# A graph-attention kernel: stores of the transformed keys by halves of the partitions, and the first loads in another order

## The chip, the cores and the metric

The kernel runs on one core of one Trainium2 chip. The metric is the time of one execution on the device in microseconds (us); shorter is better. Three executions of the kernel before were timed, with a median of 545.88 us, and one more was recorded by the hardware profiler. Every view of the trace below is of that recorded execution.

A core has TensorE (PE, matrix products; its weight loads are listed apart as PEld), VectorE (DVE), ScalarE (ACT), GpSimd (POOL) and SyncE (SP). Sixteen transfer engines move data between DRAM and SBUF, the on-chip memory, which has 128 partitions. PSUM is the memory that TensorE writes its products to. A transfer is issued by an engine (nearly all of them by SP, a few by ACT) and goes into that engine's queue; SPq and ACTq in a row mean that the issuing is meant.

## The reference

The reference is one layer of graph attention in float32, with an integer adjacency. B = 16 graphs, N = 512 nodes of F = 512 features, L = 11 labels, 16 heads of 32 features, and the first 20 nodes as neighbours. Per graph it computes this:

```
self_feat = concat(v, q, but 0 for q where a row of v sums to 0) @ W_self.T + b_self
output    = self_feat
for d in 0, 1:                                   # the adjacency and its transpose
    cond, vb = sum of A over labels, A @ w_bias + b_bias
    qh  = self_feat @ Wq[d].T + bq[d]            # 512 queries
    kh  = self_feat[:20] @ Wk[d].T + bk[d]       # 20 keys
    aff = qh . kh / sqrt(32) by heads, -9e15 where cond <= 0, + vb
    w   = softmax(aff over the 20)
    output += (w @ self_feat[:20]) @ Wout[d] by heads + bout[d]
return v + relu(output)
```

## The kernel before, in words

The kernel has a setup for all graphs (the first 92 us or so), and then a loop of 16 passes, one for each graph, whose order of work is written out as a table of steps. The change touches the setup alone.

The setup turns everything that depends on the 20 neighbours into operands that the loop only has to load. It first warms TensorE with matrix products of ones (L581, result unused), while the first loads come in. The rows of the 20 x 16 neighbours (`xkv`) and the weights of the self features (`ws_v`) come in four pieces of 128 input features, k = 0 to 3; `kv_rows(k)` issues the piece of `xkv` on SP and that of `ws_v` on ACT. The products of piece k (`kv_terms`, L637) write four PSUM banks (ps_kv twice, ps_u, ps_v in the profile). The query's part follows (L656), then the keys' features (`key_rows`, L693), of which the differences to neighbour 0 are kept in `khD`.

Then come the **bursts**. `keys(runs)` multiplies the query weights into the keys (L790), so that the loop can multiply self features by the outcome without forming queries. The outcome has 16 stages, numbered `at_g`. A stage is collected in a tile `st` of 128 partitions x 2,128 float32 (14 graphs x 152); the first two graphs' part goes to another tile, `g01`, and stays on the chip. ACT (L811) and DVE (L813) evict the PSUM tiles of a burst into `st`. The pool has four `st` tiles, so the evictions of stage k use the tile of stage k - 4. When a stage is complete, SP stores it to DRAM with one transfer (`g_d`, L816). Each partition's 8,512 bytes are contiguous in DRAM. The loop loads its graph's part back from there (`load_keys`, L137).

Between the bursts, `plan` puts the values' products (`values`, L759, stored at L767 to `vw_d`), the masks of graph 0, the row sums, and the first feature products (L277). The engines get their instructions in the order of the program text, and each executes its own in that order, with semaphores between the engines. Transfers of one queue are also issued in order. The semaphores for transfers come in eight lanes that are used in turn, so a transfer that is issued waits for the landing of the one eight before it.

At the end of the setup its pools are given back, and the loop's tiles take over their memory: the sums of keys (L394, on POOL), for instance.

Of the kernel before, what the change touches and what calls it, by code (L numbers as in the profile page):

```python
# [14 lines left out]
P = 128  # L15
# [4 lines left out]
def gat_kernel(  # L20
# [20 lines left out]
    nc = tc.nc  # L41
# [13 lines left out]
    HA = 2  # L55
    RA = P // HA
# [6 lines left out]
    HF = F // 2  # L63
# [16 lines left out]
    def bank(name, at=0):  # L80
        if at % C > 1:
            return (ps_u, ps_v)[at % C - 2]
        return acc["pool"].tile([P, 512], F32, tag="acc", name=name)
# [3 lines left out]
    ws_v = const.tile([P, C, F], F32, name="ws_v")  # L87
# [13 lines left out]
    g_d = dram.tile([C * C, P, B - 2, WD // C], F32, name="g_d")  # L101
# [304 lines left out]
    def score_product(b, n):  # L406

        rows, keys, to = {
            1: (lambda: self_block(b, 0, 0), lambda: key_block(b, 0), ps_a),
            2: (lambda: self_block(b, 0, 1), lambda: key_block(b, 1), ps_w),  # L410
            3: (lambda: sums[b, "s", 4], lambda: key_block(b, 2), ps_e),
            4: (lambda: self_block(b, 1, 1), lambda: sums[b, "t", 4], ps_a),
            5: (lambda: sums[b, "s", 1], lambda: sums[b, "t", 1], ps_e),
            6: (lambda: sums[b, "s", 2], lambda: sums[b, "t", 2], ps_a),
            7: (lambda: sums[b, "s", 3], lambda: key_block(b, 3), ps_a),
        }[n]
        rows, keys, to = rows(), keys(), grid(to).rearrange("p j (x m) -> p j x m", m=NG)
        for k in range(2):
            for j in range(C):
                for a in range(HA):  # L420
                    nc.tensor.matmul(  # L421
                        to[bass.ts(a, RA), j, :, 1:], rows[:, k, bass.ts(j, RA)],
                        keys[:, k, a].rearrange("p (x m) -> p x m", m=ND),
                        start=False, stop=k == 1, skip_group_check=True,
                    )
# [118 lines left out]
    with tc.tile_pool(name="setup", bufs=1) as sp, tc.tile_pool(  # L544
# [6 lines left out]
        q_sb = sp.tile([P, C, B], F32, name="q_sb")  # L551
        bs_sb = sp.tile([P, C], F32, name="bs_sb")
# [11 lines left out]
        with tc.tile_pool(name="setup_k", bufs=1) as sk:  # L564
            xkv = sk.tile([P, C, BM], F32, name="xkv")
# [11 lines left out]
                nc.gpsimd.memset(mean[bass.ts(q, 32), q], 1.0 / 32)  # L577

            warm = bank("ps_warm")
            for _ in range(7):  # L580
                nc.tensor.matmul(warm[:, :P], ones, ones, start=True, stop=True)  # L581

            def rows(sb, src, queue=nc.sync):
                queue.dma_start(sb, src.rearrange("(c p) f -> p c f", p=P))

            def kv_rows(k, queue=nc.sync):
                rows(xkv[:, k : k + 1], xkvT[bass.ts(k, P)])
                rows(ws_v[:, k : k + 1], wsT[bass.ts(k, P)], queue)
# [9 lines left out]
                    wq[d].rearrange("(a l p) f -> p a l f", l=2, p=P)[:, :, l],  # L598
                )

            for k in range(3):
                kv_rows(k, nc.scalar)
                if k == 1:
                    nc.sync.dma_start(q_sb, qT)
            nc.scalar.dma_start(bs_sb, b_self)
            nc.scalar.dma_start(bk_sb, bk)
            nc.scalar.copy(nzk[:, :1], ones[:, :1])
            rows(xkv[:, 3:], xkvT[bass.ts(3, P)])
# [114 lines left out]
        with tc.tile_pool(name="setup_g", bufs=4) as sg:  # L723
# [55 lines left out]
            def keys(runs):  # L779


                pairs = [ps_s.tile([P, 2, 512], F32, tag="s", name=f"ps_g{runs[0]}{i}") for i in range(2)]
                at = 0
                for at_g, d, lo, hi in runs:
                    fc, hg = ORDERED[at_g]
                    n = (hi - lo) * ND
                    for hl in range(HL):
                        r = bass.ts(hl, DH)
                        for a in range(HA):
                            nc.tensor.matmul(  # L790
                                pairs[hl // 2][bass.ts(a, RA), hl % 2, at : at + n],
                                wq_sb[r, d, hg, bass.ds(fc * P + a * RA, RA)],
                                khD[r, d * C + hg, lo * ND : hi * ND], start=True, stop=True,
                            )
                    at += n
                at = 0
                for at_g, d, lo, hi in runs:
                    n = (hi - lo) * ND
                    if at_g not in stages:
                        stages[at_g] = sg.tile([P, B - 2, HL, 2, ND], F32, tag="st", name=f"st{at_g}")  # L800
                    st = stages[at_g]
                    for half in range(2):
                        of = pairs[half][:, :, at : at + n].rearrange("p h (b m) -> p h b m", m=ND)
                        to = st[:, max(lo - 2, 0) : hi - 2, bass.ts(half, 2), d].rearrange("p b h m -> p h b m")
                        evictions = [(to, of[:, :, max(2 - lo, 0) :])]
                        if lo == 0:
                            to = g01[:, :, at_g].rearrange("p b (h d m) -> p h b d m", d=2, m=ND)
                            evictions.append((to[:, bass.ts(half, 2), :, d], of[:, :, :2]))
                        for to, of in evictions:
                            if half == 0:  # L810
                                nc.scalar.activation(to, of, AF.Copy, scale=SCALE)  # L811
                            else:
                                nc.vector.tensor_scalar(to, of, SCALE, None, ALU.mult)  # L813
                    at += n
                    if d == 1 and hi == B:
                        nc.sync.dma_start(g_d[at_g], st)  # L816

            def features(n):
                if n == 1:
# [33 lines left out]
            for n, runs in enumerate(bursts):  # L853
                for i in range(len(rest)):
                    if i < (4 if n == 0 else 1) or any((d, ORDERED[at_g][1]) == rest[0] for at_g, d, _, _ in runs):
                        key_rows(*rest.pop(0))
                keys(runs)
                if 0 < n < 5:
                    for d in range(2):
# [422 lines left out]
```

## Time and profile before

| what | value |
|---|---|
| timed runs | 545.64, 545.88 and 546.28 us (median 545.88) |
| the recorded execution | 546.29 us, of which its span is 544.5 us |
| granted TensorE clock | 0.995 |
| busy in the span | PE 537.3 us, DVE 455.9, POOL 430.9, ACT 369.2 |
| stores of stages | 16 of 1,064 KB, issued from 29.4 to 86.5 us |

A row of the timeline reads: start in us, duration in us, engine, line, operation, output<-inputs, how many of them, and in brackets the idle time before it with what ended it. A row of the waits reads: engine, tile and line, what it waited for, us in total, how often, the longest. A row of the windows gives the stretch, its length, the busy time of PE, PEld, DVE, ACT and POOL (with the number of instructions), then the clock, the share of time for which the 16 transfer engines were busy on average, and GB/s. A row of a queue (q1 is SP's, q8 TensorE's instructions) has packets, MB and the share of the 16 engines' time.

### The profile page before, as it was taken

What the parts mean: (1) busy time and instruction counts of PE and PEld (TensorE: products, weight loads), DVE (VectorE), ACT (ScalarE), POOL (GpSimd) and SP (SyncE); (2) the same over time, 40 slices, a digit from 0 to 9 for tenths busy, and PEclk for the clock granted to TensorE, in tenths of its full rate; (3) what the DMA queues carried; (4) which work ended last, traced back from release to release, by engine and by line L of the source; (5) the groups of instructions that cost most, each with busy time, mean ns of one, the idle gap of its engine ahead of it and who ended that gap; (6) DMA issues with size and microseconds to landing.
All of it is one profiled execution on the core that took longest, in us unless ns stands there. A gap on an engine that the chain in (4) does not pass through costs nothing.

```text
span 544.5 us, 19552 instructions
## 1 busy us (share of the span) xinstructions
PE 537.3 (99%) x8136; PEld 415.4 (76%) x8136; DVE 455.9 (84%) x773; ACT 369.2 (68%) x804; POOL 430.9 (79%) x379
## 2 busy tenths in 40 slices
PE   9999999999999999999999999999999999999996
PEld 5444446988797979797978788887879797979794
DVE  0588674899989898989898988989898989898986
ACT  1145444767786869695968686968777786867554
POOL 3215906859797979797979798998979797979795
PEclk9999999999999999999999999999999999999998
DMA  8998989795575858585766656666657575745025
GB/s 296 396 413 332 362 330 330 230 304 171 184 234 185 260 171 266 169 245 194 221 222 187 235 179 216 213 196 213 195 200 234 195 248 182 224 128 172 23 79 194
DMA packets 87400, 122.90 MB, mean 226 GB/s; under 512 B 11656, under 2 KB 56208, under 8 KB 85264
## 3 DMA queue, kind: packets, MB, share of 16 engines
q1 hardware_dynamic: 86304, 120.47, 66.7%
q8 instruction: 64, 1.05, 0.8%
q10 hardware_dynamic: 1008, 1.19, 0.6%
q14 instruction: 24, 0.20, 0.1%
HBM read 84.99 MB, written 37.95 MB: 226 GB/s over the span
## 4 chain that ended last, share of the span: by engine, by line
PE 97%; DMA 0%; DVE 0%; POOL 0%; issue 0%; ACT 0%; DVEq 0%; POOLq 0%
PE ps_a L421 23%; PE ps_u L277 20%; PE ps_v L277 15%; PE ps_e L421 11%; PE ps_w L421 6%; PE ps_w L513 6%; PE ps_v L759 4%; PE ps_k L693 2%; PE ps_a L988 2%; PE ps_kv L637 1%; PE ps_e L513 1%; PE ps_v L693 1%; PE ps_u L693 1%; PE ps_warm L581 1%; DMA out_T<-o 0%; PE ps_u L637 0%
## 5 line engine op out<-in xcount | busy, mean ns | idle before, releaser
L485 POOL TENSOR_TENSOR s<-s,sm 128x640 f32<-128x640 f32 x60 | 76.3, 1274 | 40.4 <-DVE sm L481 40.3
L342 ACT ACTIVATE prod<-adj,wb_sb 128x160 f32<-128x160 int32 x165 | 80.5, 586 | 0.6 <-DMA adj<-in_adj 0.6
L538 POOL TENSOR_TENSOR o<-o,x 128x512 f32<-128x512 f32 x59 | 75.3, 1279 | 0.8 <-ACT o L1120 0.8
L476 ACT ACTIVATE s<-s 128x640 f32<-128x640 f32 x60 | 42.4, 730 | 25.4 <-DVE s L472 25.4
L277 PE MATMUL ps_u<-t,ws_s 128*64 128x246 f32 x480 | 55.0, 370 | 0.0
L449 DVE TENSOR_TENSOR u<-ps_a,both 128x640 f32<-128x640 f32 x30 | 24.7, 823 | 28.7 <-PE ps_a L421 28.7
L480 DVE TENSOR_REDUCE sm<-s 128x32 f32<-128x640 f32 x60 | 47.7, 796 | 0.0
L394 POOL TENSOR_TENSOR k<-g,k 128x608 f32<-128x608 f32 x30 | 44.0, 1488 | 1.1
L404 POOL TENSOR_TENSOR s<-sf 128x512 f32<-128x512 f32 x30 | 37.8, 1277 | 6.5 <-DVE sf L315 5.6
L277 PEld LDWEIGHTS ps_u<-t,ws_s 128*64 128x64 f32 x480 | 34.0, 137 | 11.7
L491 DVE STREAM_TRANSPOSE wt<-s 128x512 f32<-128x512 f32 x60 | 41.3, 689 | 0.1
L366 ACT COPY both<-add 64x160 f32<-64x160 f32 (+1 forms) x68 | 21.5, 316 | 24.1 <-DVE add L355 23.5
L243 POOL TENSOR_TENSOR t<-x 128x492 f32<-128x492 f32 x30 | 37.3, 1244 | 0.0
L394 POOL TENSOR_TENSOR k<-g 128x608 f32<-128x608 f32 x15 | 22.3, 1486 | 18.6 <-DMA g_d<-st 18.6
L513 PE MATMUL ps_e<-wt,vd 32*32 32x256 f32 (+1 forms) x600 | 36.6, 389 | 0.0
L513 PE MATMUL ps_w<-wt,vd 32*32 32x256 f32 (+1 forms) x600 | 36.6, 389 | 0.0
L315 DVE TENSOR_TENSOR sf<-ps_v,f 128x492 f32<-128x492 f32 x45 | 30.0, 667 | 6.7 <-PE ps_v L277 5.9
L347 DVE TENSOR_REDUCE cond<-adj 128x160 f32<-128x1760 int32 (+1 forms) x17 | 31.1, 1829 | 4.3 <-DMA adj<-in_adj 4.3
L243 POOL TENSOR_TENSOR t<-x,t 128x492 f32<-128x492 f32 x30 | 34.6, 1152 | 0.2
L421 PEld LDWEIGHTS ps_a<-g,sf 128*64 128x64 f32 x480 | 30.3, 137 | 5.6 <-issue 5.4
L175 ACT ACTIVATE xn<-xn 128x512 f32<-128x512 f32 x56 | 34.5, 618 | 0.0
L355 DVE TENSOR_REDUCE add<-prod 128x160 f32<-128x1920 f32 (+1 forms) x17 | 34.5, 2028 | 0.0
(366 smaller groups left out, 1516.8 us busy)
## 6 DMA issues: line engine op xcount, KB each, us to landing
g_d<-st SPq DMA_DIRECT2D x16, 1064.0 KB
g<-g_d SPq DMA_DIRECT2D x56, 304.0 KB
out_T<-o SPq DMA_DIRECT2D x60, 256.0 KB
xn<-in_xn SPq DMA_DIRECT2D x28, 512.0 KB
x<-in_xT SPq DMA_DIRECT2D x28, 512.0 KB
adj<-in_adj SPq DMA_DIRECT2D x32, 440.0 KB
nz<-nz_d SPq DMA_DIRECT2D x16, 256.0 KB
vd<-bd_d SPq DMA_DIRECT2D x64, 64.0 KB
```

Of the source, the lines that this page charges most:

```text
L243: nc.gpsimd.tensor_sub(t, one, two)
L277: nc.tensor.matmul(to[bass.ts(a, RA), bass.ts(i, HN)], lhs, x[:, k], start=n in starts and (i, k) == (0, 0), stop=k == 1, skip_group_check ...
L342: nc.scalar.activation(label_sums(b)[:, :, l], labels(b)[:, :, l], AF.Copy, scale=wb_sb[:, l : l + 1])
L394: op(t, one(), two())
L404: op(t, one(), two())
L421: nc.tensor.matmul(to[bass.ts(a, RA), j, :, 1:], rows[:, k, bass.ts(j, RA)], keys[:, k, a].rearrange("p (x m) -> p x m", m=ND), start=Fals ...
L476: nc.scalar.activation(t, t, AF.Exp)
L480: nc.vector.tensor_reduce(sm, rows_of(b, i, l), AX.X, ALU.add)
L485: nc.gpsimd.tensor_mul(t, t, us.pop((b, "sum", i, l)).unsqueeze(2).to_broadcast([P, 32, NG]))
L491: nc.vector.transpose(wts[b][:, i, l, : W * 4 // 5], t[:, :, :MW])
L513: nc.tensor.matmul((ps_w, ps_e)[a][to, g, bass.ts(c, NH)].rearrange("p (i j n) -> p i j n", i=2, n=32), lhs, rhs, start=False, stop=True, ...
L538: nc.gpsimd.tensor_add(t, t, xs[b][:, c])
```

## The change

There are three edits. One warming matrix product is dropped (7 become 6). The first loads are written out in another order: piece 0 of `xkv`, piece 0 of `ws_v` in two halves of its columns, the query `q_sb` and the bias `bs_sb`, and then pieces 1 and 2; before, `q_sb` came after piece 1 and `bs_sb` after piece 2. And each stage is stored by two transfers of 64 partitions each (HA is 2, RA is 64, HF is 256). Lines move by two or three: L637 becomes L639, L790 becomes L792, L816 becomes L819.

```diff
--- before.py
+++ after.py
@@ -577,7 +577,7 @@
                 nc.gpsimd.memset(mean[bass.ts(q, 32), q], 1.0 / 32)
 
             warm = bank("ps_warm")
-            for _ in range(7):
+            for _ in range(6):
                 nc.tensor.matmul(warm[:, :P], ones, ones, start=True, stop=True)
 
             def rows(sb, src, queue=nc.sync):
@@ -598,11 +598,13 @@
                     wq[d].rearrange("(a l p) f -> p a l f", l=2, p=P)[:, :, l],
                 )
 
-            for k in range(3):
+            rows(xkv[:, :1], xkvT[:P])
+            for h in range(2):
+                rows(ws_v[:, :1, bass.ts(h, HF)], wsT[:P, bass.ts(h, HF)], nc.scalar)
+            nc.sync.dma_start(q_sb, qT)
+            nc.scalar.dma_start(bs_sb, b_self)
+            for k in (1, 2):
                 kv_rows(k, nc.scalar)
-                if k == 1:
-                    nc.sync.dma_start(q_sb, qT)
-            nc.scalar.dma_start(bs_sb, b_self)
             nc.scalar.dma_start(bk_sb, bk)
             nc.scalar.copy(nzk[:, :1], ones[:, :1])
             rows(xkv[:, 3:], xkvT[bass.ts(3, P)])
@@ -813,7 +815,8 @@
                                 nc.vector.tensor_scalar(to, of, SCALE, None, ALU.mult)
                     at += n
                     if d == 1 and hi == B:
-                        nc.sync.dma_start(g_d[at_g], st)
+                        for a in range(HA):
+                            nc.sync.dma_start(g_d[at_g, bass.ts(a, RA)], st[bass.ts(a, RA)])
 
             def features(n):
                 if n == 1:
```

What moves at the start on ACT, which issues the loads of `ws_v`. Before:

```order
L584 DMA ws_v<-in_wsT 128x512 x3
L605 DMA bs_sb<-in_b_self 128x4
L606 DMA bk_sb<-in_bk 128x8
L607 ACT_TABLE_LOAD
L607 COPY nzk<-ones 128x1
```

With the change:

```order
L584 DMA ws_v<-in_wsT 128x256 x2
L605 DMA bs_sb<-in_b_self 128x4
L584 DMA ws_v<-in_wsT 128x512 x2
L608 DMA bk_sb<-in_bk 128x8
L609 ACT_TABLE_LOAD
L609 COPY nzk<-ones 128x1
```

The first load is now two of half the columns, and the small `bs_sb` stands ahead of pieces 1 and 2. On SP `q_sb` likewise moves from behind the second piece of `xkv` to behind the first.

The last stores on SP, ahead of the loads of graph 1's adjacency (`adj`), of its rows (`xn`) and of the label bias (`cq`). Before:

```order
L816 DMA g_d<-st_1133 128x2128
L767 DMA vw_d<-ws_q 128x4x128
L816 DMA g_d<-st_1183 128x2128
L816 DMA g_d<-st_1225 128x2128
L767 DMA vw_d<-ws_q 64x4x128 x2
L816 DMA g_d<-st_1271 128x2128
L125 DMA adj_1377<-in_adj 128x880 x2
L119 DMA xn_0_1380<-in_xn 128x1024
```

With the change:

```order
L819 DMA g_d<-st_1145 64x2128 x2
L769 DMA vw_d<-ws_q 128x4x128
L819 DMA g_d<-st_1196 64x2128 x2
L819 DMA g_d<-st_1239 64x2128 x2
L769 DMA vw_d<-ws_q 64x4x128 x2
L819 DMA g_d<-st_1286 64x2128 x2
L125 DMA adj_1393<-in_adj 128x880 x2
L119 DMA xn_0_1396<-in_xn 128x1024
```

Nothing changes places here; each store is issued twice, and what follows stands behind two transfers.

## The prediction

> **What bounds the kernel now.** I read the page first (shares of the engines, then the chain that ended last), then the waits of TensorE, then the stretches in which TensorE stands.
>
> ```profile
> span 544.5 us, 19552 instructions
> PE 537.3 (99%) x8136; PEld 415.4 (76%) x8136; DVE 455.9 (84%) x773; ACT 369.2 (68%) x804; POOL 430.9 (79%) x379
> PE 97%; DMA 0%; DVE 0%; POOL 0%; issue 0%; ACT 0%; DVEq 0%; POOLq 0%
> PE ps_a L1065 <- DVE wt L1029: 1.6, 1, 1.6
> PE ps_warm L581 <- DVE ones L569: 1.0, 1, 1.0
> PE ps_v L759 <- issue: 0.9, 1, 0.9
> ```
>
> TensorE is busy for 99% of the span and makes up 97% of the chain. Its three visible waits sum to 3.5 us. So a change that leaves TensorE's work alone can win very little, but it loses, one for one, every microsecond for which TensorE has to stand. All three edits lie in the setup, the first 92 us or so; nothing after it is touched.
>
> One of the three waits is of use here. It is put down to "issue", so no semaphore ended it:
>
> ```profile
> 62.15 1.91 PE L759 MATMUL ps_v<-wo_sb,kvT 128*32 128x512 f32 x12
> 64.95 1.05 PE L759 MATMUL ps_v<-wo_sb,kvT 128*32 128x512 f32 x4 [0.89 <-issue]
> 65.93 0.29 PE L790 MATMUL s_g(10, 0, 12, 16)0_1030<-khD,wq_sb 32*64 32x76 f32 x4
> 69.79 1.92 PE L759 MATMUL ps_v<-wo_sb,kvT 128*32 128x512 f32 x16
> 71.64 0.48 PE L790 MATMUL ps_g(12, 0, 0, 16)0_1115<-khD,wq_sb 32*64 32x304 f32 x4
> ```
>
> The same sixteen records take 1.85 us from 69.79 to 71.64, but 3.78 us from 62.15 to 65.93: 1.93 us are lost in the middle of a group. TensorE's own instructions come through a transfer queue too, and the records show one block of them arriving just then:
>
> ```profile
> q8 instruction: 64, 1.05, 0.8%
> 0.00:64.90 64.90, 63.02 (x1102) 30.93 (x1103) 39.31 (x107) 23.06 (x72) 28.89 (x36) 1.00 0.97 360
> 36.40:92.15 55.75, 54.86 (x979) 26.69 (x970) 39.38 (x104) 25.14 (x81) 26.73 (x23) 1.00 0.91 343
> ```
>
> These are 64 blocks of 16 KB (1.05 MB). The last two rows end in the share of time for which the 16 transfer engines worked, and in GB/s: 0.97 up to the stall, and 0.91 at 343 GB/s from the first key store's bytes (36.40) to the last one's landing (92.15), as the packets' records have them. I read the lost 1.93 us as TensorE running out of instructions because their block was held up by full transfer engines. The second row says what matters most below: **in the stretch of the key stores the transfer engines are nearly as full as TensorE.**
>
> **The stores in halves.** Sixteen stores of 1,064 KB become 32 stores of 64 partitions each. There are two costs. The issuing cost comes first:
>
> ```profile
> L816 SPq DMA_DIRECT2D g_d<-st x16: 319/320/1032, 29.4 to 86.5; - x16
> 29.36 10.84 SPq L816 DMA_DIRECT2D g_d<-st  x4
> 86.47 1.03 SPq L816 DMA_DIRECT2D g_d<-st  x1
> 87.55 1.39 SPq L125 DMA_DIRECT2D adj<-in_adj  x2
> ```
>
> Sixteen more issues at 0.32 us are 5.1 us of SP, spread over 57 us in which SP mostly waits. At the end, where adj queues right behind the last store, it is one more issue: 0.32 us on a transfer that the last store holds up for longer. I cost it at nothing; without that cover it is 0.3 us.
>
> The other cost is the rate at which half of the partitions can be read. No g_d store of this shape is in the trace, but the values' store at L767 exists in both shapes: one transfer from 128 partitions at 55.11, and at 84.86 two transfers of 64 partitions that together hold as many bytes.
>
> ```profile
> 55.11 0.39 SPq L767 DMA_DIRECT2D vw_d<-ws_q  x1
> 84.86 1.33 SPq L767 DMA_DIRECT2D vw_d<-ws_q  x2
> 58.25:58.75 0.50, 0.50 (x32) 0.42 (x30) 0.50 (x1) 0.27 (x1) 0.50 (x1) 1.00 1.12 335
> 86.25:87.25 1.00, 1.00 (x14) 0.68 (x12) 0.59 (x3) 0.02 (x1) 0.48 (x1) 1.00 0.77 208
> q1 hardware_dynamic: 334, 0.17, 112.1%
> q1 hardware_dynamic: 374, 0.21, 76.8%
> ```
>
> The windows are the inside of the two transfers (they wait in the queue before that), and the queue rows belong to them in the same order: packets, MB, share of 16 engines' time. From 128 partitions a 512-byte packet takes 1.121 x 0.5 us x 16 / 334 = 26.8 ns and the total is 335 GB/s. From two times 64 it takes 0.768 x 1.0 us x 16 / 374 = 32.9 ns and the total is 208 GB/s, although both halves of the partitions are in the queue together. What the g_d store does now, in a window in its middle:
>
> ```profile
> DMA packets 79, 0.67 MB, mean 448 GB/s; under 512 B 0, under 2 KB 0, under 8 KB 0
> q1 hardware_dynamic: 79, 0.67, 107.4%
> ```
>
> A packet (one row of a partition, 8,512 bytes) takes 1.074 x 1.5 us x 16 / 79 = 0.326 us, 26.1 GB/s per engine. A store is 8 such rounds, 2.61 us.
>
> The factor on these 2.61 us is what I don't know. **Low end 1.22**, the ratio of the packet times (32.9 / 26.8). **High end 2.01**: if 208 GB/s over 16 engines, 13.0 each, is a limit of the half, 26.1 / 13.0. **Between, 1.67**: if an engine reads half of the partitions at 512 B / 32.9 ns = 15.6 GB/s, then 26.1 / 15.6. I take 1.67. The large packets ask for more per engine than the small ones do (26.1 against 512 B / 26.8 ns = 19.1 GB/s), so a narrower way to the partitions must hit them harder than 1.22; and 208 GB/s holds gaps (76.8% busy) that a full queue would close. Nothing excludes 1.0 outright, if the engines drift apart so that some work on one half and some on the other; that is a rival.
>
> [...]
>
> Now the room. The stretch of 55.75 us holds 0.91 x 55.75 = 50.7 us of transfer time; the stores are 16 x 2.61 = 41.7, the rest 9.0. At 1.67 the stores need 69.7 us, with the rest 78.7: **the stretch grows by 78.7 - 55.75 = 23.0 us**. (Break-even is (55.75 - 9.0) / 41.7 = 1.12.) For 1.22 it is 50.9 + 9.0 - 55.75 = 4.1 us, for 2.01 it is 37.1.
>
> **How it reaches TensorE.** The pool of staging tiles has four. ScalarE and VectorE evict stage k only when the store of stage k - 4 has landed, and TensorE's bursts stand behind them with two PSUM buffers. At 78.7 / 16 = 4.9 us per store, the twelfth store lands four stores before the end, 92.15 + 23.0 - 19.6 = 95.5. Stage 15's burst at L790 runs now at 84.08, so it comes 11 us later at the least. The rest of the delay comes at the seam to the loop:
>
> ```profile
> 84.08 0.32 PE ps_g(15, 0, 6, 16)0_1292 L790 x4
> 86.77 1.48 POOL L394 TENSOR_TENSOR k<-g 128x608 f32<-128x608 f32 x1 [18.56 <-DMA g_d<-st]
> 92.82 2.24 PE L421 MATMUL ps_a<-k,s 128*64 128x152 f32 x32
> 94.44 5.35 ACT L342 ACTIVATE prod<-adj,wb_sb 128x160 f32<-128x160 int32 x11 [0.58 <-DMA adj<-in_adj]
> 94.45 1.99 DVE L347 TENSOR_REDUCE cond<-adj 128x160 f32<-128x1760 int32 x1 [4.29 <-DMA adj<-in_adj]
> ```
>
> POOL's k goes into memory that the staging tiles held, so it waits for stores; it ends at 88.25 and TensorE needs it at 92.82: 4.6 us of slack. ScalarE and VectorE both stand for adj, which is queued behind the last store, and everything later on these two engines stands behind them. So the whole growth arrives, less about these 4.6 us: **23.0 - 4.6 = 18.4 us**. For 1.22 the 4.1 us vanish in the slack; for 2.01 it is 32.5.
>
> **The first loads and the warming.**
>
> ```profile
> 1.04 3.36 PE ps_warm L581 x14
> 4.40 2.29 PE ps_kv L637 x16
> 4.87 0.20 PEld L637 LDWEIGHTS ps_kv<-xkv,ws_v 128*32 128x32 f32 x4 [0.34 <-issue]
> 5.40 0.20 PEld L637 LDWEIGHTS ps_kv<-xkv,ws_v 128*32 128x32 f32 x4 [0.34 <-issue]
> 7.38 0.93 PEld L637 LDWEIGHTS ps_kv<-xkv,ws_v 128*32 128x32 f32 x16
> 8.46 0.12 PEld L637 LDWEIGHTS ps_u<-xkv,ws_v 128*32 128x32 f32 x4
> ```
>
> Seven warming matmuls are 14 passes in 3.36 us, so one fewer takes 2 x 0.24 = 0.48 us off the front, if the data are there. Groups of four go at a pitch of 0.53 us (4.87 to 5.40) and later at 0.27 (7.38 to 8.46 holds four groups): TensorE runs at half speed up to about 6.7 us. If the full speed comes at the same time as now, what moves forward is half-speed work and the gain is 0.24 us; if the data come later than the seventh matmul would have ended, it is nothing. I take 0.2 (0 to 0.48). The weights in two loads take one issue more on ScalarE's queue; q_sb and bs_sb move ahead of the k = 1 loads by one small transfer each. The later products stand in line behind ps_kv, which takes over 2 us, and I cost this at nothing; uncovered it is one issue, 0.3 us.
>
> **The sum.** The profiled execution took 546.29 us, of which 544.5 are span. 546.29 + 18.4 - 0.2 = 564.5; the median of the runs, 545.88, is 0.4 below that execution, so 564.1. The 1.93 us of the late instruction block are not taken off: while the stores set the pace, TensorE stands in that place anyway. With 1.5 (a little above the middle of 1.22 and 1.67) and 2.01 for the ends, the sum is 545.88 + (62.6 + 9.0 - 55.75 - 4.6) - 0.2 = 557 and 545.88 + 32.5 - 0.2 = 578: the case's own range.
>
> **The rivals.** (A) *Faster: the halves cost no bandwidth and let the instruction block in.* Engines drift apart over 32 small stores, both halves are read at once, and shorter stores leave gaps for the block at 62. Then 545.88 - 1.93 - 0.2 = 543.8. For it: the stall is plainly there, and the queue is full up to it. Against: in the trace's pair of 64-partition stores both halves were queued and the total stayed at 208 GB/s. (B) *The halves cost little (below 1.22) and the stall stays or moves*: 545.88 - 0.2 = 545.7, no change. For it: the low end of the bounds and the slack of 4.6 us. (C) *Slower at the start:* if the weights come after six matmuls have ended, TensorE stands, and the full speed, reached 5.6 us after the first matmul now (1.04 to 6.7), has to be earned from 4.0 on, up to 9.6: half of 2.9 us is lost, 545.88 + 1.5 = 547.4. It decides from a gap of any length only if the speed forgets that fast; the trace has no gap there to tell.
>
> **Chances.** Stores set the pace (the forecast) 0.56; A 0.27; B 0.12; C 0.05. What a measurement of this kernel can tell from no change is about 0.2%, 1.1 us. Faster is A and a little of B: 0.28. Same is the rest of B: 0.11. Slower is the forecast and C: 0.61. The range has to hold A at its low end and the forecast up to its high factor: 543.4 to 578; left out are some 0.04 below and 0.08 above.
>
> **What would show it.** The packets of the g_d stores: 0.33 us as now (A, B) or about 0.54 (forecast); GB/s in the stretch of the stores: 343 or nearer 240; the last store's landing: 92 or about 115; waits of ScalarE and VectorE for a staging tile, and of TensorE for PSUM at L792, none now. The group at 62 us shows A: 1.85 us instead of 3.78. The first pitch of 0.27 us shows C: at 6.7 or later. The forecast is wrong if the packets of half stores stay below 0.37 us.

## The result

The changed kernel takes 565.29 us (median; 564.72 to 566.76) against 546.15 for the kernel before in the same comparison: a ratio of 1.0357 with a 95% interval of 1.0346 to 1.0369, so it is **3.57% slower**. 564.1 was forecast. The profiled execution has a span of 563.5 us, 19.0 more than before. The page of the changed kernel, its waits of TensorE, and its windows of two stretches (the first is the one that was shown of before; the second goes to the landing of the last key store, which comes at 109.44 instead of 92.15):

```profile
span 563.5 us, 19576 instructions
PE 540.8 (96%) x8134; PEld 420.3 (75%) x8134; DVE 455.9 (81%) x773; ACT 369.6 (66%) x804; POOL 430.6 (76%) x379
PE 87%; DMA 5%; SPq 3%; ACT 1%; DVE 1%; issue 1%; POOL 1%; ACTq 0%; DVEq 0%; POOLq 0%
PE ps_a L421 <- DVE u L449: 7.4, 1, 7.4
PE s_g(14, 0, 12, 16)0_1252 L792 <- ACT g L813: 1.8, 1, 1.8
PE ps_g(13, 1, 3, 16)0_1217 L792 <- ACT g L813: 1.7, 1, 1.7
PE ps_g(11, 0, 6, 16)0_1091 L792 <- ACT g L813: 1.3, 1, 1.3
36.40:92.15 55.75, 48.17 (x852) 22.90 (x844) 34.78 (x94) 23.07 (x74) 21.40 (x18) 0.97 0.92 271
36.40:109.44 73.04, 64.58 (x1074) 35.33 (x1066) 38.98 (x102) 27.32 (x82) 31.16 (x26) 0.98 0.92 268
```

TensorE has 3.5 us more of busy time (540.8 against 537.3) and 15.5 us more of idle time. The transfer engines are as busy as before in the stretch of the stores (0.92 against 0.91), but move 271 GB/s instead of 343. The waits that are new are those that the prediction named: the bursts at L792 for the evictions (the ones shown sum to 4.8 us), and one of 7.4 us at the seam to the loop.

Where the seam's wait comes from stands in the timeline:

```profile
113.10 5.26 ACT L342 ACTIVATE prod<-adj,wb_sb 128x160 f32<-128x160 int32 x11 [9.87 <-DMA adj<-in_adj]
113.11 1.99 DVE L347 TENSOR_REDUCE cond<-adj 128x160 f32<-128x1760 int32 x1 [13.58 <-DMA adj<-in_adj]
115.01 0.81 DVE L449 TENSOR_TENSOR u<-ps_a,both 128x640 f32<-128x640 f32 x1
115.97 4.21 PE L421 MATMUL ps_a<-g,s 128*64 128x152 f32 x32 [7.42 <-DVE u L449]
88.94 3.32 PE L277 MATMUL ps_v<-early_t,ws_s 128*64 128x246 f32 x16
88.94:92.20 3.26, 3.26 (x21) 1.63 (x17) 1.54 (x5) 1.36 (x5) 0.00 (x0) 0.54 0.99 282
115.97:119.90 3.93, 3.92 (x32) 3.93 (x34) 2.24 (x3) 3.90 (x10) 3.19 (x4) 0.50 0.20 24
```

The same two groups of products in the kernel before:

```profile
99.02 2.24 PE L421 MATMUL ps_a<-g,s 128*64 128x152 f32 x32
81.20 1.88 PE L277 MATMUL ps_v<-early_t,ws_s 128*64 128x246 f32 x16
```

ScalarE and VectorE stand for adj until 113.1 (94.44 before). VectorE's next instruction frees the PSUM bank that TensorE waits for. The two TensorE rows at 115.97 and 88.94 show something that the prediction didn't have: 32 matrix products in 4.21 us and 16 in 3.32, where before the same ones took 2.24 and 1.88. The clocks of the two windows, 0.50 and 0.54, say why: after the waits TensorE ran at half speed for some microseconds. That is 2.0 + 1.4 = 3.4 us, nearly the whole growth of the busy time (3.5).

### The profile page after: what moved, and what is told of

It reads as the page before. It is cut to its first block, busy times and chain, and to the rows that moved or that the text cites. A ratio compares the mean times of both kernels' runs of the same rounds, so it can differ in the third digit from the quotient of the medians.

```text
span 563.5 us, 19576 instructions
## 1 busy us (share of the span) xinstructions
PE 540.8 (96%) x8134; PEld 420.3 (75%) x8134; DVE 455.9 (81%) x773; ACT 369.6 (66%) x804; POOL 430.6 (76%) x379
## 4 chain that ended last, share of the span: by engine, by line
PE 87%; DMA 5%; SPq 3%; ACT 1%; DVE 1%; issue 1%; POOL 1%; ACTq 0%; DVEq 0%; POOLq 0%
PE ps_a L421 22%; PE ps_u L277 18%; PE ps_v L277 14%; PE ps_e L421 11%; PE ps_w L513 5%; PE ps_w L421 5%; DMA g_d<-st 2%; PE ps_k L695 2%; PE ps_a L991 1%; DMA nz<-nz_d 1%; PE ps_v L761 1%; SPq L819 1%; DMA xn<-in_xn 1%; PE ps_e L513 1%; DMA ws_v<-in_wsT 1%
## 5 line engine op out<-in xcount | busy, mean ns | idle before, releaser
L277 PE MATMUL ps_u<-t,ws_s 128*64 128x246 f32 x480 | 55.0, 370 | 0.0
L277 PEld LDWEIGHTS ps_u<-t,ws_s 128*64 128x64 f32 x480 | 34.4, 137 | 11.4
L421 PE MATMUL ps_a<-g,s 128*64 128x152 f32 x480 | 35.5, 303 | 7.4 <-DVE u L449 7.4
L421 PEld LDWEIGHTS ps_a<-g,s 128*64 128x64 f32 x480 | 33.0, 143 | 7.7 <-issue 7.7
```

The lines of the kernel that those rows point to most:

```text
L277: nc.tensor.matmul(to[bass.ts(a, RA), bass.ts(i, HN)], lhs, x[:, k], start=n in starts and (i, k) == (0, 0), stop=k == 1, skip_group_check ...
L421: nc.tensor.matmul(to[bass.ts(a, RA), j, :, 1:], rows[:, k, bass.ts(j, RA)], keys[:, k, a].rearrange("p (x m) -> p x m", m=ND), start=Fals ...
```

## The experiments

The theory was that a transfer from the lower or the upper half of the partitions finds only half of the ways out of SBUF. The main rival was the mere number of transfers (issues, the eight semaphore lanes, SP); a second one was the new order of the loads.

### Which edit costs the time

The loads alone: each stage stored whole, the rest as in the change.

```diff
-                        for a in range(HA):
-                            nc.sync.dma_start(g_d[at_g, bass.ts(a, RA)], st[bass.ts(a, RA)])
+                        nc.sync.dma_start(g_d[at_g], st)
```

> The loads in the new order and six warming products, but whole stores. Theory (the halves of the partitions cost the time): the loss is gone, 545 to 546.2 us, that is 0 to 0.8 below before, and the instruction stall near 62 us is there as before (about 1.9 us). Rival (the new order of the loads costs part of it): above 548. The start edits by themselves, read from the changed kernel's trace, put the keys' first products 0.41 us earlier, so the theory's own number is 0.4 below before.

546.67 us against 545.79, ratio 1.0010 (0.9997 to 1.0023). The loss is gone. The 0.4 us of gain didn't come either (the median is 0.5 us above the band that was expected), and no difference can be told. The wait near 62 us stayed, as expected.

The stores alone, on the kernel before:

```diff
-                        nc.sync.dma_start(g_d[at_g], st)
+                        for a in range(HA):
+                            nc.sync.dma_start(g_d[at_g, bass.ts(a, RA)], st[bass.ts(a, RA)])
```

> The loads and the warming as before, each stage stored as two stores of 64 partitions. Theory: the whole loss and no more, before + 19 to 20 us (565 to 566). Rival (loss shared with the loads): less than before + 15.

565.25 us, ratio 1.0347 (1.0317 to 1.0378): the whole loss. The loads play no measurable part.

### Number of transfers, number of partitions, or which partitions

Two stores of all 128 partitions, each with half of the columns:

```diff
-                            nc.sync.dma_start(g_d[at_g, bass.ts(a, RA)], st[bass.ts(a, RA)])
+                            at_b = bass.ts(a, (B - 2) // HA)
+                            nc.sync.dma_start(g_d[at_g, :, at_b], st[:, at_b])
```

> The change, but the two stores of a stage split it by graphs (columns of the tile): 128 partitions x 4,256 bytes each, so as many transfers and bytes as in the change. Theory (what costs is that a transfer sees half of the partitions): packets of 4,256 bytes take about 0.16 us, last store lands near 92 us, time 543.5 to 546. Rival (the number of transfers costs: issuing, waits for the eight lanes, SP): near the change, 560 to 566.

Two stores of 64 partitions, every second one:

```diff
-                            nc.sync.dma_start(g_d[at_g, bass.ts(a, RA)], st[bass.ts(a, RA)])
+                            nc.sync.dma_start(g_d[at_g, a::HA], st[a::HA])
```

> The change, but the two stores of a stage take the even and the odd partitions: 64 partitions x 8,512 bytes each as in the change, spread over the whole height. Theory A (the lower 64 and the upper 64 partitions have separate ways, and a transfer of one of them has half the ways): no loss, packets 0.33 us, 543.5 to 546. Theory B (any transfer of 64 partitions is slow, whichever they are): near the change, 560 to 566, packets up to 0.65 us. Rival (number of transfers): near the change as well, with packets of 0.33 us.

The halves of the columns took 546.96 us (1.0026; 1.0008 to 1.0043), every second partition 546.56 (1.0010; 0.9999 to 1.0021). Both have as many transfers as the change and lose at most 1.2 us (the first, 1.0 us above the band that was expected, has a new wait of 1.8 us for graph data early in the loop, at 117.8 us, which the second hasn't; the second is 0.6 us above its band). So it isn't their number. The second has the same 64 rows of 8,512 bytes too, so it isn't the number of partitions. The only thing left is which partitions stand in one transfer.

To see the price without mixing, both stores of a stage read the lower half (the upper one is left out):

```diff
-                            nc.sync.dma_start(g_d[at_g, bass.ts(a, RA)], st[bass.ts(a, RA)])
+                            nc.sync.dma_start(g_d[at_g, bass.ts(a, RA)], st[:RA])
```

> The change, but both stores of a stage read the lower 64 partitions; the upper half is left out, bytes and transfers are as in the change. Theory (the halves have separate ways, and in the change some engines have drifted on to the other half, which is why a third of its packets are still fast): here no packet finds a free way, all go at 0.65 us, and the sum of the prediction with a factor of 2.01 holds, 576 to 580. Rival (the engines' drift plays no part): as the change, 563 to 567.

582.15 us, a single time, 2 above the top of what was expected, and far from the rival. Both its stores write the same addresses of DRAM as those of the change and differ only in the partitions they read, so the 17 us between the two kernels come from the reading side. The transfers inside the stores, from a view of DMA packets for a window each; first the lower half twice from 45 to 51 us, then every second partition from 75 to 79, then the changed kernel from 41 to 43 and from 59.5 to 61.5:

```profile
DMA packets 182, 1.25 MB, mean 209 GB/s; under 512 B 35, under 2 KB 35, under 8 KB 35
q1 hardware_dynamic: 182, 1.25, 99.7%
```

```profile
DMA packets 251, 1.71 MB, mean 428 GB/s; under 512 B 51, under 2 KB 51, under 8 KB 51
q1 hardware_dynamic: 250, 1.69, 101.4%
```

```profile
DMA packets 122, 0.83 MB, mean 417 GB/s; under 512 B 25, under 2 KB 25, under 8 KB 25
q1 hardware_dynamic: 121, 0.82, 102.0%
DMA packets 49, 0.42 MB, mean 209 GB/s; under 512 B 0, under 2 KB 0, under 8 KB 0
q1 hardware_dynamic: 49, 0.42, 106.3%
```

The engines are busy all the time in all four. With the lower half alone they move 209 GB/s, with every second partition 428. The change does **both**: at 41 to 43 us, when half-stores of several stages are queued, 417 GB/s; at 59.5 to 61.5, when only the two halves of one stage are queued (issued from 58.22 to 59.32), 209. By the packets in order of their start, the first 512 (eight half-stores, from 34.70 to 47.57 us) are 95% fast, and of the 64 from 59.33 on none is. Of the 2,048 packets of 8,512 bytes, these shares are fast (under 400 ns) and of double length (600 to 700 ns), with the mean:

| kernel | fast | double | mean ns |
|---|---|---|---|
| before | 0.93 | 0.02 | 342 |
| every second partition | 0.96 | 0.01 | 334 |
| the change | 0.57 | 0.24 | 458 |
| lower half twice | 0.13 | 0.79 | 620 |

Most packets are either as fast as ever or twice as long (four in five with the change, nine in ten with the lower half twice). That fits two engines sharing one way out when both read the same half, and not sharing it once one of them has run ahead into the other half. That two engines share a way and drift apart like this is a reading: these records don't say which engine moved which packet. And 13% of the packets are fast with the lower half alone too, where no store reads the other half, so not all of the 57% (a third, by the expectation of that run) are due to drift.

Could the two halves be kept apart on purpose, in two queues? The upper half was issued by ScalarE:

```diff
-                            nc.sync.dma_start(g_d[at_g, bass.ts(a, RA)], st[bass.ts(a, RA)])
+                            (nc.sync, nc.scalar)[a].dma_start(g_d[at_g, bass.ts(a, RA)], st[bass.ts(a, RA)])
```

> The change, but the upper half of each stage is issued by ScalarE, so the two halves stand in two queues at the same time. Theory (two engines get in each other's way only while both read the same half): if the engines take from both queues in turn, both halves are read at once, packets of 0.33 us become the rule, and most of the loss is gone: 547 to 556, the rest being ScalarE's waits at the issue. Rival (transfers of one core follow each other whatever the queue): as the change, 563 to 567.

561.04 us (1.0276; 1.0261 to 1.0291): a miss for the theory's number, and 2 below the rival's band. The share of fast packets rose only to 0.64 (mean 441 ns). Halves issued together still moved in part one behind the other, as those of stage 4: issued at 48.60 and 48.94 us, they moved from 49.74 to 52.65 and from 52.48 to 54.77. Why they did is open. And TensorE has three waits that no semaphore ended:

```profile
PE ps_v L277 <- issue: 2.6, 1, 2.6
PE ps_g(6, 0, 12, 16)1_805 L792 <- issue: 2.2, 1, 2.2
PE ps_g(4, 1, 9, 16)0_684 L792 <- issue: 1.7, 1, 1.7
```

By the packets' records each of the three ends 1.4 to 1.5 us after a block of TensorE's instructions has landed. A second data queue isn't needed for this: with the lower half twice, on one queue, TensorE waits at two of the same places.

```profile
PE ps_g(6, 0, 12, 16)1_805 L792 <- issue: 1.9, 1, 1.9
PE ps_g(4, 1, 9, 16)0_684 L792 <- issue: 0.7, 1, 0.7
```

So late blocks go with slow half-stores too. How much of them the second queue adds wasn't tested apart.

### The wait near 62 us, and where its gain went

In the changed kernel and in all runs with smaller stores, the wait inside this group of products is gone; in the runs with whole stores it is there. The rows are of the kernel with every second partition, and then of the one with whole stores and new loads:

```profile
62.46 1.92 PE L761 MATMUL ps_v<-wo_sb,kvT 128*32 128x512 f32 x16
```

```profile
63.16 1.92 PE L761 MATMUL ps_v<-wo_sb,kvT 128*32 128x512 f32 x14
66.03 1.02 PE L761 MATMUL ps_v<-wo_sb,kvT 128*32 128x512 f32 x2 [0.96 <-issue]
```

The packets' records say what ends it. After the first 40 us, the thirteen profiles hold nine waits of TensorE's products that are put down to "issue", and each ends 1.2 to 1.5 us after a block of its instructions has landed (in the kernel before, 63.54 and 64.95). With every second partition that block starts at 56.77 us instead of 62.59, and nothing waits for it.

Yet the time didn't fall by 1.9 us. With the loads and the warming as before, and every second partition:

```diff
-                        nc.sync.dma_start(g_d[at_g], st)
+                        for a in range(HA):
+                            nc.sync.dma_start(g_d[at_g, a::HA], st[a::HA])
```

> The kernel before with one edit: each stage stored as two stores of the even and of the odd partitions; loads and warming as before. Theory: the instruction stall near 62 us is gone (1.5 to 1.9 us), but at the seam to the loop the loads of graph 1 land no earlier, TensorE waits there, and the total is within 1 us of before. Against the same stores with the new loads (0.8 us above before) this gives what the loads cost: 0.3 to 0.8 us. Rival (the gain at 62 us stays to the end): 544 or less.

546.31 us against 546.11 (1.0009; 0.9994 to 1.0025), no difference, as expected. Where it goes shows at the seam, first this kernel, then the same one with graph 1's adj issued ahead of the last store and its cq ahead of graph 2's xn:

```profile
94.19 5.36 ACT L342 ACTIVATE prod<-adj,wb_sb 128x160 f32<-128x160 int32 x11 [1.92 <-DMA adj<-in_adj]
94.20 1.99 DVE L347 TENSOR_REDUCE cond<-adj 128x160 f32<-128x1760 int32 x1 [5.63 <-DMA adj<-in_adj]
98.89 0.53 POOL L438 TENSOR_TENSOR cqd<-cq 128x160 f32<-128x160 f32 x1 [3.87 <-DMA cq<-cq_d]
100.58 1.88 PE L277 MATMUL ps_u<-t,ws_s 128*64 128x246 f32 x16 [0.91 <-POOL t L243]
```

```profile
91.20 1.99 DVE L347 TENSOR_REDUCE cond<-adj 128x160 f32<-128x1760 int32 x1 [3.49 <-DMA adj<-in_adj]
91.31 5.37 ACT L342 ACTIVATE prod<-adj,wb_sb 128x160 f32<-128x160 int32 x11
94.67 0.53 POOL L438 TENSOR_TENSOR cqd<-cq 128x160 f32<-128x160 f32 x1 [0.47 <-DMA cq<-cq_d]
```

```diff
+                        if at_g == C * C - 1:
+                            for h in range(HA):
+                                load_adj(1, h)
                         for a in range(HA):
                             nc.sync.dma_start(g_d[at_g, a::HA], st[a::HA])
...
-        1: "Lx1 Lx2 Lxn1 Lxn2 rs12 rs34 fl Snz Lnz Lk11 Lk21 Lk22 Lt3",
+        1: "Ladj1 Ladj2 Lx1 Lx2 Lxn1 Lxn2 rs12 rs34 fl Snz Lnz Lk11 Lk21 Lk22 Lt3",
...
+        Lxn1:2/reluE:-2 Lxn2:2/reluE:-2
```

> As the last one (even and odd partitions, start as before), and graph 1's adj loads are issued before the last stage's store, its label bias (cq) before graph 2's rows (xn). Theory (what gives the gain of 62 us back is that adj and cq land behind the last store): adj lands 2 us or more earlier, the waits at the seam go, and the whole 1.5 to 1.9 us stay: 543.8 to 544.6. Rival (the seam is held by something else, by the store of the last stage itself, or by POOL): within 0.5 us of the kernel without this edit.

With the loads where they were, adj lands as late as in the kernel before (94.2 against 94.4) and cq 0.7 us later (98.89 against 98.17). TensorE starts the group of L421 that is shown above at 97.43 instead of 99.02, and the next group of L277 at 100.58 instead of 101.08: of the 1.6 us that it was ahead, 0.9 go into a wait for POOL's t, which stands behind cq. Moved, adj lands 3 us earlier and cq 4.2. This kernel took 545.56 us against 546.11 (0.9986; 0.9970 to 1.0001), less of a gain than was expected. It was run again beside the same edit with whole stores:

> The kernel before with whole stores; graph 1's adj is loaded ahead of the last stage's store, cq ahead of graph 2's xn. Theory (the seam only binds once TensorE arrives there earlier, as it does when the stall near 62 us is gone): no change, within 0.6 us of before, the stall near 62 us still there. Rival (the seam costs time by itself): 0.8 us or more below before.

> Even and odd partitions, start as before, adj and cq earlier: the same kernel again, beside the one with whole stores. Theory (the gain near 62 us needs the smaller stores, and the earlier adj and cq keep it): 0.8 to 2 us below the kernel with whole stores and below before. Rival (the 2 us of the one profile are its luck with TensorE's first microseconds): within 0.4 us of both.

With whole stores 545.98 us (0.9998; 0.9987 to 1.0008), with every second partition **544.93 against 546.27 (0.9977; 0.9965 to 0.9988)**. The edit at the seam alone gives nothing and the smaller stores alone give nothing; both together gave 0.6 us in the first comparison, which is not clear of noise, and 1.3 in the second, which is. Its span in the profile is 542.3 us, against 544.0 with whole stores. So this version beats both kernels, by little. The edit moves adj and cq together; which of the two counts wasn't tested.

The same edit at the seam on the stores by lower and upper halves asks whether the last part of the loss comes through adj:

> Stores by lower and upper partitions as in the change (start as before), with adj ahead of the last stage's store and cq ahead of xn. Theory (the last part of the loss, from +9 to +19 us, comes through adj, on which ScalarE and VectorE stand): adj lands about 4 us earlier, and the time falls by 3 to 5 us, to 560 to 562. Rival (the seam is held by the memory of the staging tiles, which POOL and the loop's tiles take over): 564 to 566.

561.79 us (1.0288; 1.0250 to 1.0326), inside the theory's band. TensorE's wait at the seam shrank:

```profile
PE ps_a L421 <- DVE u L449: 4.1, 1, 4.1
```

From 7.4 to 4.1 is 3.3 us, and the time fell by 3.5 (565.25 to 561.79, on two chips, four times each, so that size is rough). In the profiles adj is there 4.5 us earlier than with the halves alone (108.83 against 113.32), and TensorE's waiting group starts 4.5 us earlier (111.69 against 116.18). So the trace shows the chain from the last store over adj to TensorE.

## Why the prediction was right, point by point

**The mechanism** held: the lower half of the partitions alone moved at half the rate of every second partition (209 against 428 GB/s), the stores set the pace (the last one landed at 109.44 us instead of 92.15), and ScalarE and VectorE carry the delay to TensorE by the staging tiles (the waits at L792 that are shown, 4.8 us) and by adj (the one of 7.4). The packets of half-stores took 0.458 us on average, above the 0.37 that would have spoken against the forecast. The order of the chances held too. Rival A's premise, that the engines drift on to different halves, fits the 57% of packets that are fast at most; the rest was enough for the loss. Rival C didn't come: the changed kernel is at full speed from 3.9 us on (its first 16 products, at 3.90, take 1.28 us; before, from 4.33, they took 2.36).

**The factor on a store** was mis-sized. 1.67 was taken. From the windows, (0.92 x 73.04 - 9.0) / 41.7 = 1.40 came out; the mean of the packets gives 458 / 342 = 1.34. The low and the high end both rest on one short pair of half-transfers, and what was not weighed is how much is queued. A pure half costs 2.0 (209 against 417 to 428 GB/s), as the high end had it; the long queue at 41 to 43 us, with 417, costs little. So the stretch grew by 17.3 us (109.44 - 92.15), not by 23.0. (The first packet of a key store in the kernel before starts at 33.75 us, not at 36.40. That misreading leaves 90 of the 2,048 packets out of the window and hardly moves the sum.)

**From the last store to adj**, the sum had no growth. But adj came 18.7 us later (113.10 - 94.44), 1.4 more than the last store. Its own packets took 174 ns each instead of 146; why is open.

**The slack at the seam** was mis-sized the other way: 4.6 us was taken from POOL's k. It was adj that bound: TensorE's waiting group came 16.95 us later (99.02 to 115.97), so 1.7 us of the 18.7 were slack.

**Half speed after the waits** was not in the sum at all. Only the 2.0 us of the group behind the seam (clock 0.50) add to the time. The 1.4 us at 88.94 (clock 0.54) lie ahead of the seam, where TensorE had to wait in any case.

**The total** came out well by luck as much as by the mechanism. Along this path, the terms are off by -5.7 (the stretch), +1.4 (to adj), +2.9 (the slack) and +2.0 (half speed), and the 0.2 us of gain at the start, which lies ahead of the same wait, is lost. That is +0.8: 18.2 us were forecast and the span grew by 19.0. The forecast of the time missed by 1.2 us, but it is better in its total than in its terms.

**The wait near 62 us**: rightly read as a late instruction block, by the landings told above. That full transfer engines held it up is argued: the wait inside this group went with the whole stores in every run. That its 1.93 us would not show in the total was right for the change. Rival A's sum took them off in full, and that was wrong: without the loss from the halves, the time didn't fall either (1.0009 and 1.0010).

**The start**: a gain of 0.2 us was taken. The first products began at 3.90 instead of 4.33, and then waited 0.5 us for the next piece of the weights, a delay that the prediction had costed at nothing. The pair of runs with every second partition, new loads (1.0010) and old ones (1.0009), shows no difference.

**Issuing** was costed at 0.32 us each. It took more here:

```profile
L819 SPq DMA_DIRECT2D g_d<-st x32: 445/1044/2297, 29.0 to 102.8; - x32
```

The median is 1.04 us instead of 0.32. With every second partition it is 0.59 us, and that kernel loses nothing by it, so this is not where the time went.

## What to carry to other kernels

When a transfer is divided, let each part take every second partition, or half of the columns, rather than the lower or the upper half of the partitions: a lone half went at 209 instead of 428 GB/s here. (Every second partition showed no loss, columns one of 1.2 us.) Before a gain on the engine that is busy for 99% is counted, look for the next point at which something else must have arrived; 1.9 us were only worth something (0.6 and 1.3 us in two comparisons) once the loads behind the last store were moved as well. And where a change makes TensorE wait, look at the clock that it is granted afterwards: here it was 0.50 from 115.97 to 119.90, behind a wait of 7.4 us, and that cost 2.0 us.

## What was not expected of the hardware

TensorE ran at half speed after two waits of 1.75 and 1.81 us that ended 5 us apart (at 82.80 and 87.75; 16 products in 3.32 us at 88.94, clock 0.54) and after the one of 7.4 us (clock 0.50 from 115.97 to 119.90). A single wait of 1.84 us, in the run with halves of the columns, was followed by no half speed (the 16 products behind it, at 117.81, took 1.88 us). And its first microseconds differ between kernels with the same start. With the old start, before runs at half pace up to 6.7 us (its first 16 products take 2.36 us), and the kernel with every second partition does its first 16 products at full pace:

```profile
4.28 1.28 PE L637 MATMUL ps_kv<-xkv,ws_v 128*32 128x320 f32 x16
```

With the new start it is the other way: the changed kernel is at full pace from 3.90 (1.28 us), and the one with every second partition isn't:

```profile
3.90 2.36 PE L639 MATMUL ps_kv<-xkv,ws_v 128*32 128x320 f32 x16
```

This is about 1 us, and nothing in the programs differs there. Over the profiles, by the granted clock, full speed comes between 4.17 and 6.68 us with the old start and between 3.88 and 6.91 with the new one; what sets the moment was not shown. That limits what can be said of the dropped warming product: the first 16 products of one and the same start took 1.28 us in one profile and 2.36 in another.

Transfers of 64 partitions were not slow as such. Every second partition, 8,512 bytes each, went as fast as all 128 (mean packet 334 and 342 ns).
